# Two modes chains in turn, loads in source order, stores by POOL, and the residual made beside the first images

## The chip, the cores and the metric

The kernel runs on one core of a Trainium2 chip. The metric is the device time of one execution in microseconds; lower is better. Engines are TensorE (PE, with its weight loads as PEld), VectorE (DVE), ScalarE (ACT), GpSimd (POOL), and SyncE (SP), which here only issues DMAs. [...]

## The reference, cut to what matters

Two layers over an input of 256 x 256 x 128. Layer 0 is attention over rows; its result is x1, kept in DRAM as x1d. Layer 1 treats every one of 256 tokens as an image of 256 x 128 pixels (b*C tokens, H, W), and is a Fourier neural operator:

```python
attn = fno_layer(attn, p_wr, p_wi, p_bias, p_sw, p_sb, (H, W))
attn = instance_norm(attn + tokens, attn_norm_w, attn_norm_b)
attn = attn.reshape(b * (C // TOKEN_CODIM), TOKEN_CODIM, H, W)
h0 = instance_norm(attn, norm2_w, norm2_b)
h1 = fno_layer(h0, mix_wr[0], ..., norm=True, act=True)
h2 = fno_layer(h1, mix_wr[1], ..., norm=True)
out = instance_norm(h2, mon_w, mon_b) + attn
...
x = x + _L1_conv_ref(_gn(x), ...)
```

In the kernel's words: y is the unnormalized attn, an image per token; `lam` is its normalization's scale. Each fno_layer of the mixer is a spectral part (few Fourier modes: a transform, a product with weights, a transform back) and a skip part (a 4 x 4 channel mix). The first gives h1 with a Gelu ("first images"), the second h2. The output is `x1 + lam*y + kap*(h2's sums) + c0`, with kap and c0 from the statistics of h2.

## The kernel before, in words

Tokens are 256; on 128 partitions they make two halves, a = 0 and 1. Pixels of an image (32768) are cut into 16 blocks of NB = 2048, and these into 32 half blocks (units) of HB = 1024. `blocks` (16 tiles `hb[b]`) holds one half's whole image set in SBUF, 16 MB; it is used for half 0 first and for half 1 after that. Everything else goes through DRAM: x1d, `yd` (y), and mode tensors Gd0, Gd1, Gd2 (modes that are transformed back along one axis) and Yd (images that are transformed forward along one axis).

The parts, as Python generators or functions, each with `yield`s so that two can be woven:

- `y_blocks(a)` (L1280): for each unit u: load x1 of both halves (two 512 KB DMAs, tile `xt`, three slots in pool `xp`), for each even u the modes `gs` (four DMAs of Gd0); eight matmuls with `mpT` and the small `image` matmuls into four PSUM banks (`yps`); DVE scales them out (L1304) to `hb` (half 0) or a tile `yt` (half 1) and takes statistics (L1306); POOL stores y to yd (L1308) for half 1 and for b < 4 of half 0.
- `first_modes(a)` (L1374): DVE aggregates y's statistics, a chain of small operations makes lam, rho and sig; F (y's modes, from Fyd) is scaled; `mix_modes` multiplies with the weights (DVE products `x0m`, PE accumulates in `x0acc`), normalizes; `synth_modes` makes Gd1 in four chunks: matmuls `g10gp` into four banks, eviction by ACT and DVE to a tile `gt`, four stores of 256 KB to DRAM (L586, by SP).
- `first_images(a)` (L1411): for each block b: load modes `gs` (L1199), for half 1 also y (L1426, 1 MB); `ups` = skip + image matmuls, Gelu by ACT to `hb[b]` (L1446); then for block b-1: transposes `htps`, copies to `hT` (three by DVE at L1465, one by ACT at L1456), `sps` = skip of the second layer, of which DVE takes statistics (L1474), `psA` = transform along the width, copy by ACT, store to Yd (L1480, by SP). For half 0, `keep_y` stores y of blocks 4 to 15 to yd by POOL (L1432, 1 MB each) before `hb[b]` is overwritten.
- `second_modes(a)` (L1484): load `YT` from Yd in four chunks, transform (`f1ps`, L1513), `mix_modes` (`z0m`, `z0acc`), `synth_modes` to Gd2, then kap and c0 (`cvps`, L1535 to L1554).
- `second_images(a)` (L1556), the output blocks: load y, x1 (two DMAs of 512 KB each) and modes; `h2ps` = skip + image; ACT applies kap and c0 (L1583) in place; DVE makes x1 + lam*y (L1587) and adds hb (L1590); POOL stores to the output (L1591).

[...]In the mixer two pools of four are open at a time, so `ups` and `h2ps` share four, and `htps`, `sps` and `psA` share four.

The order at the end of the kernel (L1596 to L1635): y of half 0; first modes of half 0 woven with the first part of y of half 1; first images of half 0; second modes of half 0 woven with the rest of y of half 1; first modes of half 1 woven with output blocks of half 0; first images of half 1 woven with the rest of these; second modes of half 1; output blocks of half 1. `weave(main, side)` takes steps of the side generator when the numbers that main yields exceed those of the side.

`tc.manual_schedule(engines=COMPUTE)`: PE, ACT, DVE and POOL run their instructions in the order of the source; the order of SP's DMA issues is left to the scheduler, with its own estimate of due times. [...] A tile of a pool with `bufs=n` and one tag takes the n slots in turn; a load into a slot waits until its last user is done.

Of the kernel before, what the change touches and what calls it, by code (L numbers as in the profile page):

```python
# [10 lines left out]
FP = mybir.dt.float32  # L11
# [501 lines left out]
def layer1(tc, I, C, ident, x1d, upool, U, stats2, mv2, out):  # L513
# [9 lines left out]
    with ExitStack() as ctx:  # L523
# [16 lines left out]
        def synth_modes(pool, psum, Z, T, Gd, tag, spare=None, turned=False, chunk=None, ptag="s", gbufs=2):  # L540
# [4 lines left out]
            for c in range(4) if chunk is None else (chunk,):  # L545
                for part in range(1 if both else 2):
# [35 lines left out]
                    for ri in range(2) if both else (part,):  # L582
                        for jp in range(2):
                            k = 2 * ri + jp if both else jp
                            r0 = 16 * ri + 4 * c
                            nc.sync.dma_start(  # L586
                                Gd[r0 : r0 + 4, 2 * jp : 2 * jp + 2].rearrange("f j g t -> (j g) f t"),
                                gt[:, :, k * T : (k + 1) * T],
                            )
# [575 lines left out]
        END = 0.6  # L1165
# [52 lines left out]
        def flush(stage):  # L1218

            while next(stage, END) != END:  # L1220
                pass

# [7 lines left out]
        with tc.tile_pool(name="psb", bufs=4, space=PSUM) as psa, tc.tile_pool(name="spb", bufs=1) as spb:  # L1230
# [3 lines left out]
            ch4 = sp.tile([4, 6], FP, name="ch4")  # L1234
# [13 lines left out]
            for l in range(2):  # L1248
                s4 = sp.tile([4, 4], FP, name=f"s4_{l}")
# [4 lines left out]
                r4 = sp.tile([P, 4], FP, name=f"r4_{l}")  # L1254
# [14 lines left out]

        halves = []  # L1270
        for a in range(2):
# [6 lines left out]
            h.Yd = dram.tile([H, 32, P], FP, name=f"Yd_{a}")  # L1278

        def y_blocks(a, psum):  # L1280

            tt = slice(a * P, (a + 1) * P)
            for u in range(32):
                b, s = u // 2, u % 2
                xt = xts.pop((a, u)) if (a, u) in xts else load_x1(a, u)
                if s == 0:
                    gs = xp.tile([P, 4, P], FP, tag="gs", name=f"gs_{a}_{b}")
                    load_modes(gs, Gd0, b, tt)
                ps = [psum[0].tile([P, 512], FP, tag="y", name=f"yps_{a}_{u}_{j}") for j in range(4)]
# [8 lines left out]
                image(ps, gs, bsy, range(2 * s, 2 * s + 2))  # L1298
# [8 lines left out]
                if a or b < 4:  # L1307
                    nc.gpsimd.dma_start(ydv[:, a, u * HB : (u + 1) * HB], yt)  # L1308
                yield END

        def mix_modes(wp, psum, F, l, tag, out, constant=()):

# [3 lines left out]
            acc = [psum.tile([P, 512], FP, tag="q", name=f"{tag}acc_{r}") for r in range(2)]  # L1316
            by_c = [z.rearrange("p (c t) -> p c t", c=4) for z in acc]
            k = 0
            for i in range(4):
# [5 lines left out]
                for x, r, dst in ((0, "r", 0), (1, "n", 0), (0, "i", 1), (1, "r", 1)):  # L1325
                    t = wp.tile([P, 4, G, 4], FP, tag="m", name=f"{tag}m_{i}{x}{r}")
# [8 lines left out]
            sq = wp.tile([P, 2, 4, T], FP, tag="f", bufs=1, name=tag + "sq")  # L1335
# [4 lines left out]
            en = psum.tile([P, 512], FP, tag="q", name=tag + "ens")  # L1340
# [7 lines left out]
            rs = wp.tile([P, 2], FP, tag="rs", name=tag + "rs", bufs=1)  # L1348
# [4 lines left out]
            dg = wp.tile([P, P], FP, tag="m", name=tag + "dg")  # L1353
            nc.vector.tensor_scalar(dg, ident, rs[:, 0:1], None, ALU.mult)
            yield 1.8
            ps = psum.tile([P, 512], FP, tag="q", name=tag + "rsp")
# [5 lines left out]
            rsb = wp.tile([P, T], FP, tag="m", name=tag + "rsb")  # L1362
            nc.scalar.copy(rsb, ps[:, 0:T])
            Z = wp.tile([P, 4, 2, T], FP, tag="f", bufs=1, name=tag + "Z")
# [9 lines left out]
        def first_modes(a, wp, psum):  # L1374

            h = halves[a]
            F = wp.tile([P, 4, 2, P], FP, tag="F", bufs=1, name=f"F0_{a}")
# [4 lines left out]
            dg = wp.tile([P, 2, P], FP, tag="m", name=f"dg3_{a}")  # L1382
# [17 lines left out]
            ps = psum.tile([P, 512], FP, tag="q", name=f"rhops_{a}")  # L1400
            nc.tensor.matmul(ps[:, 0:256], ones, dg.rearrange("p k t -> p (k t)"), start=True, stop=True)
            yield 0.9
            rb = wp.tile([P, 256], FP, tag="m", name=f"rb_{a}")
# [7 lines left out]
            yield from mix_modes(wp, psum, F, 0, f"x{a}", z, ((sig, blk[0]), (ch[:, 2:3], ident)))  # L1411
            Z = z[0]
            for c in range(4):
                synth_modes(wp, psum, Z, P, h.Gd1, f"g1{a}", turned=True, chunk=c, ptag="q", gbufs=1)
                yield 2.7

        def first_images(a, wp, psk, pst):
# [5 lines left out]
            def load(b):  # L1423
                if a == 1:
                    ys[b] = wp.tile([P, NB], FP, tag="yt", name=f"y2_{a}_{b}")
                    nc.sync.dma_start(ys[b], ydv[:, a, b * NB : (b + 1) * NB])  # L1426
                gss[b] = wp.tile([P, 4, P], FP, tag="gs", name=f"gs2_{a}_{b}")
                load_modes(gss[b], h.Gd1, b)

            def keep_y(b):  # L1430
                if a == 0 and 4 <= b < 16:
                    nc.gpsimd.dma_start(ydv[:, a, b * NB : (b + 1) * NB], hb[b])  # L1432

            for b in range(4, 8):
                keep_y(b)
            load(0)
            for b in range(17):
                if b < 15:
                    load(b + 1)
                if b < 16:  # L1440
                    keep_y(b + 8)
                    ps = [psk.tile([P, 512], FP, tag="k", name=f"ups_{a}_{b}_{j}") for j in range(4)]
                    skip(ps, by_turn(ys.pop(b) if a else hb[b]), h.bl0, False)
                    image(ps, gss.pop(b), bs4)
                    for j in range(4):
                        nc.scalar.activation(by_turn(hb[b])[:, j], rows_of(ps[j]), AF.Gelu)  # L1446
                if b > 0:
                    turned = by_turn(hb[b - 1])
                    hT = {}
                    for j in (1, 2, 3, 0):  # L1450
                        ps = pst.tile([P, 512], FP, tag="t", name=f"htps_{a}_{b}_{j}")
# [18 lines left out]
                if b > 0:  # L1470
                    ps = [pst.tile([P, 512], FP, tag="t", name=f"sps_{a}_{b}_{j}") for j in range(4)]
# [3 lines left out]
                    psA = pst.tile([P, 512], FP, tag="t", name=f"psA_{a}_{b}")  # L1475
# [4 lines left out]
                    nc.sync.dma_start(  # L1480
# [4 lines left out]
        def second_modes(a, wp, psum):  # L1485
# [3 lines left out]
            F = wp.tile([P, 4, 2, P], FP, tag="F", bufs=1, name=f"F1_{a}")  # L1489
# [12 lines left out]
            gbufs = 1 if a == 0 else 2  # L1502
            load(0)
            yield 6.0
            for c in range(4):
                if gbufs > 1 and c < 3:
                    load(c + 1)
                ps = psum.tile([P, 512], FP, tag="q", name=f"f1ps_{a}_{c}")
# [11 lines left out]
                if gbufs == 1 and c < 3:  # L1520
                    load(c + 1)
                    yield 4.0
            z = []
            yield from mix_modes(wp, psum, F, 1, f"z{a}", z)
            Z, left = z
            for c in range(4):
                synth_modes(wp, psum, Z, P, h.Gd2, f"g2{a}", chunk=c, ptag="q", gbufs=gbufs)
                yield 2.7

            Fw = wp.tile([P, 2, P], FP, tag="m", name=f"Fw_{a}")  # L1530
            nc.vector.tensor_scalar(Fw, F[:, 0], hw0, None, ALU.mult)
            ps = psum.tile([P, 512], FP, tag="q", name=f"cvps_{a}")
# [6 lines left out]
            cv = wp.tile([P, P], FP, tag="m", name=f"cv_{a}")  # L1539
            nc.vector.tensor_mul(cv, blk[1], ps[:, 0:P])  # L1540
            yield 0.9
            ps = psum.tile([P, 512], FP, tag="q", name=f"cvps2_{a}")
# [13 lines left out]
        def second_images(a, wp, psk, bufs):  # L1556

            h = halves[a]
            lam, kap, c0 = (h.col[:, k : k + 1] for k in (3, 8, 9))
            got = {}  # L1560

            def load(b):
                xt, yt = [], []
                for s in range(2):
                    px = slice(b * NB + s * HB, b * NB + (s + 1) * HB)
                    yt.append(wp.tile([P, HB], FP, tag="yo", name=f"y4_{a}_{b}_{s}", bufs=bufs[1]))
                    nc.sync.dma_start(yt[s], ydv[:, a, px])
                    xt.append(wp.tile([P, HB], FP, tag="xo", name=f"x4_{a}_{b}_{s}", bufs=bufs[0]))
                    nc.sync.dma_start(xt[s], x1v[:, a, px])
                gs = wp.tile([P, 4, P], FP, tag="gs3", name=f"gs3_{a}_{b}")  # L1570
                load_modes(gs, h.Gd2, b)
                got[b] = xt, yt, gs

            load(0)
            for b in range(16):
                if b < 15 and bufs[1] > 3:
                    load(b + 1)
                xt, yt, gs = got.pop(b)
# [223 lines left out]
```

## Time and profile before

Three runs took 3005.37, 3007.17 and 3008.3 us. The profiled execution took 3009.91 us, with a span of 3007.9 us at a mean granted PE clock of 0.931.

| what | busy us, whole span | share |
|---|---|---|
| PE | 2638.8 | 88% |
| DVE | 2038.8 | 68% |
| POOL | 1514.7 | 50% |
| ACT | 1435.4 | 48% |
| DMA, bytes moved | 430.02 MB | mean 143 GB/s |

How to read it: these are means over parts with different limits. Layer 0 runs from the start to about 1656 us, the head of layer 1 (attention over tokens) to about 1905, and the parts named above fill the last 1100 us. A row of a table by stages has the stretch, its length, then busy time and instruction count of each engine, the granted PE clock, the busy share of the DMA engines and what they moved. A row of the chain of waits has a start, a length, and the engine and line (or the transfer) that held the end up at that time.

### The profile page before, as it was taken

To read this page: it belongs to the slowest core of one execution; us is meant where nothing else is said; L and a number is where in the kernel's file an instruction comes from. 1 tells how busy PE (TensorE), PEld (TensorE's weight loads), DVE (VectorE), ACT (ScalarE), POOL (GpSimd) and SP (SyncE) were. 2 spreads that over 40 slices of the span, in tenths; PEclk is the share of its full clock that TensorE was granted. 3 is DMA by queue.
4 is the path that set the end of the run, shared out by engine and by line. 5 is a ranking of instruction groups with operands and counts; after the bars stand their busy time and mean duration, and the time that the engine had idled before them with its cause. 6 is when DMAs were issued, how large, how long until landed. Compare 5 with 4: busy or idle time off the path is not lost. (4 is left out here: it accounts for less than half of the span.)

```text
span 3007.9 us, 70049 instructions
## 1 busy us (share of the span) xinstructions
PE 2638.8 (88%) x28526; PEld 1908.8 (63%) x28526; DVE 2038.8 (68%) x3251; ACT 1435.4 (48%) x2828; POOL 1514.7 (50%) x1174
## 2 busy tenths in 40 slices
PE   6899999999999999999999899898779866577644
PEld 6677777777777777777777467685545543333432
DVE  7788888888888888888888547465445445456354
ACT  0477777777777777777776223000132002343022
POOL 0499999999999999999999002000100000000011
PEclk9999999999999999999999899999989887788755
DMA  9422222122222221222221011885844576995499
GB/s 364 156 64 66 65 72 66 64 68 70 66 65 72 66 66 64 72 66 66 65 73 45 23 50 53 288 280 193 303 175 153 203 258 231 300 321 201 130 374 338
DMA packets 270202, 430.02 MB, mean 143 GB/s; under 512 B 26102, under 2 KB 202697, under 8 KB 262072
## 3 DMA queue, kind: packets, MB, share of 16 engines
q1 hardware_dynamic: 253176, 358.41, 35.8%
q0 software_dynamic: 16704, 67.12, 5.5%
q8 instruction: 226, 3.70, 0.5%
q14 instruction: 96, 0.79, 0.1%
HBM read 290.17 MB, written 135.27 MB: 141 GB/s over the span
## 5 line engine op out<-in xcount | busy, mean ns | idle before, releaser
L299 POOL TENSOR_TENSOR e<-e,b1T 128x1024 f32<-128x1024 f32 x256 | 606.5, 2369 | 166.1 <-PE u L348 90.5
L303 POOL TENSOR_TENSOR es<-e 128x512 f32<-128x512 f32 x512 | 639.0, 1269 | 20.1
L281 ACT ACTIVATE sc<-sc,b2T 128x512 f32<-128x512 f32 x512 | 339.0, 662 | 365.4 <-PE sc L272 357.1
L323 DVE RECIPROCAL av<-av 128x256 f32<-128x256 f32 x256 | 452.3, 1767 | 27.2 <-DVE og L322 1.4
L281 ACT ACTIVATE e<-sc,b2T 128x512 f32<-128x512 f32 x512 | 348.0, 680 | 0.0
L294 DVE TENSOR_TENSOR e<-sc,b1T 128x1024 f32<-128x1024 f32 x256 | 310.9, 1214 | 0.0
L272 PE MATMUL sc<-qkT 32*128 32x256 f32 x4096 | 294.0, 401 | 1.3 <-DVE e L294 1.3
L1591 POOL DMA_DIRECT2D out_dram<-x x64 | 34.0, 531 | 509.2 <-DVE x L1590 374.8
L1293 PE MATMUL yps<-xt,mpT 128*128 128x256 f32 x1024 | 251.7, 398 | 27.5 <-DVE yt L1304 24.5
L311 PE MATMUL av<-e,v 128*32 128x256 f32 x4096 | 274.8, 385 | 0.5 <-POOL e L299 0.5
L1308 POOL DMA_DIRECT2D yd<-yt x32 | 17.0, 531 | 479.3 <-DVE yt L1304 479.3
L272 PEld LDWEIGHTS sc<-qkT 32*128 32x128 f32 x4096 | 185.9, 185 | 112.1 <-issue 97.7
L1293 PEld LDWEIGHTS yps<-xt,mpT 128*128 128x128 f32 x1024 | 196.1, 197 | 72.2 <-DVE yt L1304 29.3
L322 DVE SCALAR_TENSOR_TENSOR og<-gate,av 128x256 f32<-128x256 f32 x256 | 107.7, 421 | 190.6 <-PE av L316 190.6
L327 POOL TENSOR_TENSOR x<-xt,bo 128x256 f32<-128x256 f32 x256 | 187.3, 732 | 0.0
L246 PE MATMUL qk<-xnT,wT_wq 128*128 128x256 f32 x512 | 179.6, 433 | 1.7 <-ACT xnT L238 1.7
L1583 ACT ACTIVATE blocks<-h2ps,col 128x512 f32<-128x512 f32 x128 | 89.1, 777 | 176.1 <-PE h2ps L1182 176.0
L252 PEld LDWEIGHTS gv<-wT_wv,kvT 128*128 128x128 f32 x1024 | 155.2, 192 | 13.2
L316 PE MATMUL av<-es,ones 128*32 128x256 f32 x2048 | 157.5, 379 | 2.5 <-POOL es L303 2.5
L333 PE MATMUL wo<-wT_wo,og 128*128 128x128 f32 x1024 | 156.9, 276 | 2.7 <-DVE og L324 2.7
L348 PE MATMUL u<-adft,x 128*128 128x129 f32 x1024 | 156.4, 275 | 0.0
L252 PE MATMUL gv<-wT_wv,kvT 128*128 128x128 f32 x1024 | 156.1, 275 | 0.0
(692 smaller groups left out, 5150.1 us busy)
## 6 DMA issues: line engine op xcount, KB each, us to landing
xt<-x1d SPq DMA_DIRECT2D x128, 512.0 KB
xb<-in_x_dram SPq DMA_DIRECT2D x32, 1024.0 KB
xt<-in_x_dram SPq DMA_DIRECT2D x128, 256.0 KB
kt<-in_L_conv_kv_x_dram SPq DMA_DIRECT2D x128, 256.0 KB
x1d<-x SPq DMA_DIRECT2D x256, 128.0 KB
y<-yd SPq DMA_DIRECT2D x64, 512.0 KB
x<-x1d SPq DMA_DIRECT2D x64, 512.0 KB
out_dram<-x POOLq DMA_DIRECT2D x64, 512.0 KB, 7.2
```

The lines of the kernel that those rows point to most:

```text
L246: nc.tensor.matmul(ps[:, 0:256], wT["wq"], xnT, start=True, stop=True)
L252: nc.tensor.matmul(ps[:, 256 + c * P : 256 + (c + 1) * P], kvT[:, c * P : (c + 1) * P], wT["wv"], start=True, stop=True,)
L272: nc.tensor.matmul(sc[h // 2][:, h % 2, c * 256 : (c + 1) * 256], qkT[p, 256 + c * P : 256 + (c + 1) * P], qkT[p, 0:256], start=True, stop ...
L281: nc.scalar.activation(r["e"][1][:, :, c, :] if hp else z, z, AF.Exp, bias=b2T[:, c, s : s + 1])
L294: nc.vector.tensor_tensor(r["e"][0].rearrange("p h c q -> p (h c q)"), r.pop("sc").rearrange("p h x -> p (h x)"), b1T[:, 0:2].rearrange("p ...
L299: nc.gpsimd.tensor_tensor(e1, e1, b1T[:, 2:4].rearrange("p h c q -> p (h c q)"), ALU.mult)
L303: nc.gpsimd.tensor_tensor(r["es"][hp], e[:, :, 0, :], e[:, :, 1, :], ALU.add)
L311: nc.tensor.matmul(ps[hd, 0:256], r["v"][:, c, hd], r["e"][h // 2][:, h % 2, c, :], start=(c == 0), stop=(c == 1),)
L316: nc.tensor.matmul(ps[32 * h : 32 * h + 32, 256:512], self.ones, r["es"][h // 2][:, h % 2, :], start=True, stop=True,)
L323: nc.vector.reciprocal(rd, rd)
L327: nc.gpsimd.tensor_tensor(r["x1"], r["x"], bc(self.bo, 1, 2), ALU.add)
L1293: nc.tensor.matmul(rows_of(ps[j]), mpT[:, sc, tt], by_turn(xt[:, sc])[:, j], start=(sc == 0), stop=False,)
```

## The change

- SP joins the manual schedule: its loads are issued in source order. Loads in `y_blocks` are written two units ahead. Stores that SP issued (Gd1, Gd2, Yd) are issued by POOL.
- x1 + lam*y of half 0 is made during its first images, for blocks b >= NW = 2: x1 is loaded (tile `xw` in the three `xt` slots), ACT scales y by lam into the tile's second half, POOL adds, and POOL stores the sum to a new DRAM tensor `wd`. `keep_y` is gone; yd of half 0 is stored for b < NW only. The output blocks of half 0 then load one w of 1 MB in place of y and x1, and DVE does one add per half block (for b < 2 as before).
- y of half 1: units 0 to 23 are woven with first modes of half 0 (weight 2.2 for 1.4), and run to the end before the first images; 24 to 31 are woven with the f1ps part of second modes of half 0.
- From there, second modes of half 0 and first modes of half 1 are stepped in turn, with no y beside them. They share the `m` (2) and `gt` (1) buffers. The first modes' synthesis is then woven with output blocks of half 0 (two chunks per block), and the first images of half 1 with the rest (weight 0.85 for 0.6). In that part y of half 1 and w share four slots of 1 MB.
- Half 1's output: y and x1 of the first NX = 5 half blocks are loaded, and x1 + lam*y made, during second modes of half 1; afterwards a load of the next half blocks is written after each output block, into five x slots and two y slots.
- `ch4`, `s4` and `r4` move from pool `sp` to `spb`.

On PE the order of instructions becomes: y of half 0; y of half 1 (24 units) with x0acc and g10gp between; 16 first images; 8 y units with f1ps; z0acc and x1acc in turn, g20gp, g11gp with two h2ps blocks, a third h2ps block; then 16 first images with 13 h2ps blocks between; f1ps to g21gp of half 1; 16 h2ps blocks.

The core of the diff (renamings of pools to `Banks` and `Tiles` are left out):

```diff
-        END = 0.6
+        NW, NX = 2, 5
...
-            ch4 = sp.tile([4, 6], FP, name="ch4")
+            ch4 = spb.tile([4, 6], FP, name="ch4")
...
+            load(lo)
+            load(lo + 1)
+            for u in range(lo, hi):
                 b, s = u // 2, u % 2
-                xt = xts.pop((a, u)) if (a, u) in xts else load_x1(a, u)
...
+                if u + 2 < hi:
+                    load(u + 2)
...
-                if a or b < 4:
+                if a or b < NW:
                     nc.gpsimd.dma_start(ydv[:, a, u * HB : (u + 1) * HB], yt)
...
+            def load_w(b):
+                for s in range(2):
+                    ys[b, s] = yp.tile([P, 2, HB], FP, tag="xt", name=f"xw_{b}_{s}", bufs=3)
+                    nc.sync.dma_start(ys[b, s][:, 0], x1v[:, a, b * NB + s * HB : b * NB + (s + 1) * HB])
...
+                    nc.scalar.activation(
+                        t[:, 1], hb[b][:, s * HB : (s + 1) * HB], AF.Identity, scale=h.col[:, 3:4]
+                    )
+                    nc.gpsimd.tensor_tensor(t[:, 1], t[:, 1], t[:, 0], ALU.add)
+                    nc.gpsimd.dma_start(wd[:, px], t[:, 1])
...
                 if b < 16:
-                    keep_y(b + 8)
...
                         nc.scalar.activation(by_turn(hb[b])[:, j], rows_of(ps[j]), AF.Gelu)
+                if a == 0 and NW <= b + 1 < 16:
+                    add_w(b + 1)
...
-                    nc.sync.dma_start(
+                    nc.gpsimd.dma_start(
                         h.Yd[16 * (b - 1) : 16 * b].rearrange("(n j) f t -> (j f) n t", j=4),
...
-        with tc.manual_schedule(engines=COMPUTE):
+        with tc.manual_schedule(engines=COMPUTE | {ENG.SP}):
...
+                U1 = 24
+                with tc.tile_pool(name="mp0", bufs=1) as wp:
+                    y1 = y_blocks(1, br, 0, U1)
+                    weave((2.2 * t for t in first_modes(0, wp, tiles(wp), bq)), y1)
                     run(y1)
+                with tc.tile_pool(name="hp0", bufs=2) as wp:
+                    run(first_images(0, wp, xp, bq, br))
+                with tc.tile_pool(name="mp1", bufs=1) as wp:
+                    y1 = y_blocks(1, br, U1, 32)
+                    m0 = second_modes(0, wp, tiles(wp), bq)
+                    weave((1.5 * t for t in iter(lambda: next(m0), None)), y1)
+                    run(y1)
+                    m1 = first_modes(1, wp, Tiles(F=(xp, "yt", 2), f=(xp, "yt", 2), m=(wp, "m", 2)), br)
+                    for _ in m0:
+                        next(m1)
+                    pools = [(xp, xp), 3, True]
+                    o0 = output_0(pools, bq)
+                    weave((t / 5.4 for t in m1), o0)
+                    pools[2] = False
+                    next(o0)
+            with tc.tile_pool(name="hp1", bufs=2) as wp, tc.tile_pool(name="op0", bufs=4) as op:
+                pools[:] = [(op, wp), 4, True]
+                weave((0.85 * t for t in first_images(1, wp, op, bq, br)), o0)
                 run(o0)
...
+                    m1 = second_modes(1, wp, tiles(wp), Banks(psq, "q"), gbufs=2)
+                    weave((0.3 for _ in m1), o1.ahead())
+                with tc.tile_pool(name="opk1", bufs=8, space=PSUM) as psk:
+                    o1.run(Banks(psk, "k"))
```

## The prediction, as put on record before the run

> **What bounds the kernel now.** I read the slices first, then the busy time of each stage, then the chain of waits and the queue's own waits in the stages that the diff rewrites. In the slices, the first 1.9 ms, attention and the head of layer 1, have 9s for PE and are untouched; the last slices, from about 1905 us, are what the diff rewrites, and PE's digits fall there:
>
> ```profile
> PE   6899999999999999999999899898779866577644
> ...
> DMA  9422222122222221222221011885844576995499
> ```
>
> The stages of that part, called B to H here, as busy time of each engine in its stretch (columns: stretch, length, PE, PEld, DVE, ACT, POOL, granted PE clock, DMA share, GB/s). A, the y blocks of half 0, fills 1905 to 2052 before them.
>
> ```profile
> 2052.00:2161.00 109.00, 89.81 (x972) 62.81 (x970) 57.41 (x138) 7.65 (x15) 6.37 (x12) 0.92 0.65 217
> 2161.00:2302.00 141.00, 117.92 (x1921) 61.69 (x1921) 70.72 (x113) 51.15 (x96) 6.84 (x13) 0.90 0.47 168
> 2302.00:2346.00 44.00, 35.62 (x452) 28.12 (x448) 18.63 (x42) 0.58 (x1) 3.19 (x6) 0.97 0.91 316
> 2346.00:2459.00 113.00, 91.42 (x740) 67.23 (x740) 56.12 (x130) 7.44 (x14) 6.37 (x12) 0.90 0.61 206
> 2459.00:2593.00 134.00, 61.97 (x1028) 35.57 (x1036) 63.48 (x95) 26.82 (x43) 7.97 (x15) 0.69 0.75 249
> 2593.00:2782.00 189.00, 148.76 (x2496) 73.53 (x2480) 109.63 (x146) 75.57 (x132) 9.56 (x18) 0.88 0.79 275
> 2782.00:2852.00 70.00, 44.35 (x596) 30.30 (x612) 23.55 (x46) 7.39 (x14) 0.00 (x0) 0.78 0.41 125
> 2852.00:3007.00 155.00, 73.90 (x1024) 44.02 (x1000) 78.63 (x75) 44.58 (x65) 17.00 (x32) 0.58 0.96 353
> ```
>
> B: first modes of half 0 beside 13 y units. C: first images of half 0. D1: the four f1ps chunks beside 6 units; D2: the rest of second modes beside 13 units. E: first modes of half 1 beside 7 output blocks; PE works 62 of 134 us, so this is a chain, not an engine. F: first images of half 1 beside 9 output blocks. G: second modes of half 1 alone. H: 16 output blocks, DMA full (0.96).
>
> E's chain of waits is DMA and SP, and SP's own waits there say why: loads wait for output stores and for the DVE add, and the Gd stores queue behind them.
>
> ```profile
> 2559.15 8.67 DMA out_dram<-x
> ...
> 2570.06 5.34 DMA Gd<-g11gt
> ...
> 2584.88 7.79 DMA gs<-Gd
> ```
>
> ```profile
> SPq L1569 <- DMA out_dram<-x: 35.8, 12, 6.4
> SPq L1567 <- DVE x L1587: 23.7, 10, 9.0
> ```
>
> F's chain, one block with an output block in it: PE waits for hstat, which waits on DVE behind the adds, which wait for ACT. From psA to psA this takes 15 us (2661.1 to 2676.0, the next one), a block without output 7.0.
>
> ```profile
> 2652.83 1.30 PE h2ps L1193 x32
> 2654.13 1.14 PE h2ps L1182 x32
> ...
> 2655.93 2.12 ACT blocks L1583 x3
> ...
> 2658.06 2.36 DVE x L1590 x2
> 2660.43 0.62 DVE hstat L1474
> ```
>
> [...]for the new 128x1024 add; the trace has 2.37 us for a TENSOR_TENSOR of that shape (L299), used here. [...]the trace has medians of 4.7 (yd<-yt) and 7.2 (out_dram, DMA full).[...]
>
> **The change, part by part** (against the profiled span, 3007.9; the three timed runs have a median of 3007.17, so no correction).
>
> 1. Start of A: ch4 and s4 now load after k_sel. Eight tiny issues at the 0.35 us of k_same and k_sel: **+3** (0 to +5). Nothing else changes in A: PE is full from 1960; two blocks of y stores fewer.
>
> 2. B has 24 y units instead of 13. A unit alone on four PSUM banks takes 4.87 us (2448.6 to 2453.5: 3.72 + 0.73 of PE and 0.5 of waiting for the DVE eviction). B began at 2049, 112 us with its first unit. Upper end: 112 + 11x4.87 = 166. Lower end: PE alone, 24x4.45 + 32 (rhops 0.6, x0acc 16, ens 2, g10gp 13) = 139. The new order puts y matmuls between all pairs of x0acc, so some of the 17 us in which PE idled fill up: 155, **+43** (+27 to +54). Gd stores move from SP to POOL, behind yd stores (0.53 us each): hidden, Gd1 isn't read until C, seven units later.
>
> 3. C. Removed: 12 yd stores of 1 MB in a burst at the start; PE lost 21.8 us there waiting for gs, queued behind them, so C without it is 141-23 = 118. Added, for 14 blocks: two x1 loads (SP), two ACT scalings of 128x1024, two POOL adds, two wd stores, and the Yd store moves behind these on POOL. ACT isn't the total bound, but its order is: both scalings stand between the gelus and the hT copy, on which the last sps quarter and psA wait. A scaling: 128x512 takes 0.58 to 0.68 here, so about 1.1; the 2.2 us push hT from 2210.9 to 2213.1 in the 6.97 us block, and psA's end by 1.6. 14x1.6 = 22. Second limit: three xt slots, each held for load 4.7 + issue 0.4 + POOL 2.4 + issue 0.5 + store 4.7 = 12.7, two per block: 8.5 us a block, against 8.6 by ACT. What queues behind a wait for a slot: on ACT the hT copy, so PE; on SP the next gs load, early enough. C = 118+22 = 140, **-1**. Lower end 118 (-23), if ACT's work fits in; upper end, see the third rival.
>
> 4. D1: 8 units and the f1ps chunks. Before, 44 us with 6 units, so 15 us of other time; 8x4.87+15 = 54, **+10** (0 to +15).
>
> 5. D2 and E. Before, 113 + 134 = 247. After: the two mode chains alternate with no y beside them. From the start: rho chain of half 1, as in B from bn_aggr to x0m, 17 us, with z0acc in it; rest of both mixes, ens and rs at PE's 1.02 us a product pair, until the first g20 chunk, about 41. Chunks share one gt buffer: evictions 1.3, four POOL issues 2.1, landing 3.6 (estimate: a 256 KB Yd store took 2.15, Gd stores 3.8 to 5.3) = 7 us each, four to 69; cvps and rsp lie beside. Then four g11 chunks, 28, plus 6 for an output block on ACT and DVE before the third eviction; then stores and gs load 10: 113. **-134** (-150 to -105). The 28 DVE multiply-adds of 1.25 us and the y loads that go from here and F are counted in this; in F they lay beside ACT's 2.8 us and were free.
>
> 6. F gets 13 output blocks instead of 9 (three stand in E). Each costs 15.1-7.0 = 8.1 more; the L1605 add stays in the same place in the chain. **+32** (+15 to +38). DMA: 16x1.5 + 13x2.25 MB in 221 us is 250 GB/s, no bound.
>
> 7. G: x1/y loads for five half blocks (5 MB) go between the YT loads on SP, and five 1.25 us adds stand in DVE's chain, before the F copies and inside the mix, where DVE has about 0.3 us of slack a product: **+6** (0 to +12).
>
> 8. H: five of 32 load pairs are gone, 5 MB at 353 GB/s, 15 us. But before, these loads began at 2852 while G's tail and the first block ran; with five x slots the next x load waits until the first output store has landed: after the gs load h2ps 2.4, ACT 3.1, adds 2.4, store 5, some 13 us. **0** (-15; +12 if two y slots slow the pace).
>
> Sum: 3+43-1+10-134+32+6+0 = **-41**: 2967.
>
> **Rivals.**
> - *It hides better.* ACT and POOL work in C fits beside PE and B runs at PE's floor: -22-16, 2929. For it: PE is full in C (94 of 94 us from 2206 to 2300) and ACT is busy for only 42 of these. Against: the order on ACT.
> - *Half given back.* The gt cycle stays at E's old pace, 10.2 us a chunk (41 us for four, 2535 to 2576): 8x3.2 = +26, and F at its upper end, +6: 2999. For it: one buffer for both chains. Against: SP's queue, which set that pace, no longer carries these stores.
> - *Slower: the ring of three slots in C.* C moves 2.6 MB a block; at 8.6 us that is 300 GB/s, as busy as D1 (0.91). With a load as slow as the 8.0 us of a queued YT load and a store of 7.2, a slot turns in 0.4+8.0+2.4+0.5+7.2 = 18.5, 12.4 us a block, C = 19+14x12.4 = 192: +52, 3019. It decides from a turn of about 17.4 us (11.6 a block, C at 181), where the gain of the rest is used up. Against: a slower ring asks for less bandwidth (2.6 MB in 12.4 us is 210 GB/s), which shortens the latencies.
> - That nothing happens is excluded: the order of instructions on all engines differs from 1905 on.
>
> **Chances.** Forecast 0.50 (2937 to 2997), hides better 0.24, half given back 0.12, ring 0.14. A measurement of this kernel can tell about 0.2%, 6 us, from no change. Faster: the first two and two thirds of the third, 0.81; same 0.06; slower 0.13. Range 2916 to 3019: below the second case's time by its own uncertain terms, up to the ring's; some 0.15 is left out.
>
> **What would show it.** First ups of half 0 at about 2207 (B); no 21.8 us gs wait and 8.6 us a block in C, with hT later on ACT; g20 and g11 chunks 7 us apart and the first ups of half 1 about 113 us after the last y unit; F at 15 us a block with output, some 220 in all; H as long as now, with DMA not full at its start. Wrong, if C's blocks are 7 or over 11 us apart, if F's output blocks cost other than 8 us, or if H shrinks by 15.

## The result, and the profile after

The changed kernel takes 3036.73 us (median of 4 runs) against 3006.84 us before: ratio 1.0102, 95% interval 1.0084 to 1.0119. It is slower; 2967 us was predicted. Run again unedited beside the last of the experiments it took 3037.05 us against 3002.45: ratio 1.0129 (1.0095 to 1.0163). The profiled span is 3033.0 us, 25.1 above the span before.

The slices after. PE's last fourteen digits were 98779866577644 before and DMA's 85844576995499: PE has gained nothing in these stages, and DMA has 98 in the last two slices, in H, where it had 99.

```profile
PE   6899999999999999999998999897898665776644
...
DMA  9322222222222222222221013786978727875498
```

The stages after, as busy time of each engine in its stretch (columns as in the prediction's table). The rows are B, C, D1, D2 with E, F, G, H; each ends with its last PE instruction, H with the span:

```profile
2050.30:2213.60 163.30, 135.06 (x1336) 101.44 (x1336) 88.29 (x202) 8.93 (x16) 24.32 (x39) 0.98 0.75 262
2213.60:2353.50 139.90, 128.10 (x1924) 59.73 (x1920) 73.30 (x118) 79.44 (x123) 93.88 (x72) 0.99 0.80 270
2353.50:2421.00 67.50, 46.54 (x512) 35.78 (x512) 21.27 (x49) 0.59 (x1) 4.51 (x8) 0.87 0.79 261
2421.00:2564.20 143.20, 85.92 (x1087) 52.01 (x1089) 62.94 (x131) 23.15 (x41) 27.64 (x39) 0.76 0.44 143
2564.20:2787.80 223.60, 165.71 (x2752) 81.09 (x2752) 98.91 (x138) 86.11 (x147) 25.36 (x41) 0.85 0.70 245
2787.80:2870.40 82.60, 47.30 (x580) 32.44 (x580) 29.42 (x52) 7.83 (x14) 12.64 (x17) 0.74 0.50 163
2870.40:3033.00 162.60, 75.49 (x1024) 44.30 (x1024) 73.26 (x72) 44.77 (x65) 17.08 (x32) 0.53 0.84 304
```

With the same boundaries on the profile before (us; misses are measured minus predicted change):

| stage | before | after | change | predicted | miss |
|---|---|---|---|---|---|
| start and A | 2049.0 | 2050.3 | +1.3 | +3 | -2 |
| B | 112.1 | 163.3 | +51.2 | +43 | +8 |
| C | 141.0 | 139.9 | -1.1 | -1 | 0 |
| D1 | 43.9 | 67.5 | +23.6 | +10 | +14 |
| D2 and E | 246.7 | 143.2 | -103.5 | -134 | +30 |
| F | 187.7 | 223.6 | +35.9 | +32 | +4 |
| G | 71.2 | 82.6 | +11.4 | +6 | +5 |
| H | 156.3 | 162.6 | +6.3 | 0 | +6 |
| sum | 3007.9 | 3033.0 | +25.1 | -41 | +66 |

What the two-chain stretch no longer carries came back elsewhere: 103.5 us gained, 110.7 paid in B, D1 and F for the y units and output blocks, 17.7 in G and H. Where the misses of D1 and E lie is in the waits. D1, on SP's order (start, duration, what was issued): after the last load for C nothing until the YT load, and x1 for the y units behind it; then PE in the same place:

```profile
2338.97 0.35 SPq L1456 DMA_DIRECT2D xw<-x1d  x1
2357.45 1.18 SPq L1531 DMA_DIRECT2D YT<-Yd  x2
2358.74 1.01 SPq L997 DMA_DIRECT2D xt<-x1d  x2
```

```profile
2352.40 1.07 PE L1513 MATMUL psA<-hT,k_bfwd 128*32 128x512 f32 x8
2368.15 1.19 PE L1316 MATMUL yps<-xt,mpT 128*128 128x256 f32 x2 [14.69 <-DMA xt<-x1d]
```

SP's own waits in D1 name the releaser (total, times, longest): the YT load waits for the last Yd store, which POOL issues at the end of C.

```profile
SPq L1531 <- DMA Yd<-yA: 17.8, 2, 14.7
```

In E the chain of waits reaches back to 2532.5 only. No wait for an output store stands ahead of the Gd stores any more, as it did before. The chain holds a wait for the shared gt buffer (the last g11 chunk is evicted when the store of the one before it has landed) and, at the end, the landing of an output store:

```profile
2532.51 7.06 DMA Gd<-g11gt
...
2539.67 1.08 ACT g11gt L581 x2
...
2553.61 3.24 DMA out_dram<-w
2556.85 0.02 SPq L1199
```

SP's waits in E say how long that last store held the first load of modes of half 1's images:

```profile
SPq L1199 <- DMA out_dram<-w: 12.5, 1, 12.5
```

On DVE in E, half 1's normalisation (rq_ve from x1ens; PE had ended x1ens at 2487.0) stands behind the last g20 eviction, which waits for gt:

```profile
2489.70 1.29 DVE L581 COPY g20gt<-g20gp 128x512 f32<-128x512 f32 x2 [6.67 <-DMA Gd<-g20gt]
2498.82 1.29 DVE L581 COPY g20gt<-g20gp 128x512 f32<-128x512 f32 x2 [7.84 <-DMA Gd<-g20gt]
2500.03 0.15 DVE L35 TENSOR_SCALAR rq_ve<-x1ens 128x1 f32<-128x1 f32 x1
```

F's chain for an output block is the one of before: ACT's four scalings, DVE's adds, hstat, psA. PE's psA takes 1.93 us here, 1.07 where PE is busy (above, end of C).

```profile
2584.38 2.78 ACT blocks L1600 x4
...
2588.32 1.22 DVE w L1605
2589.53 0.62 DVE hstat L1510
...
2590.20 1.93 PE psA L1513 x8
```

### The profile page after: what moved, and what is told of

Read it like the earlier page. It is cut to its first block, busy times and chain, and to the rows that moved or that the text cites. A ratio compares the mean times of both kernels' runs of the same rounds, so it can differ in the third digit from the quotient of the medians.

```text
span 3033.0 us, 70180 instructions
## 1 busy us (share of the span) xinstructions
PE 2657.6 (88%) x28526; PEld 1909.9 (63%) x28526; DVE 2004.9 (66%) x3223; ACT 1466.3 (48%) x2856; POOL 1661.2 (55%) x1310
## 5 line engine op out<-in xcount | busy, mean ns | idle before, releaser
L252 PEld LDWEIGHTS gv<-wT_wv,kvT 128*128 128x128 f32 x1024 | 155.0, 192 | 13.4
L311 PEld LDWEIGHTS av<-e,v 128*32 128x32 f32 x4096 | 107.0, 109 | 76.1 <-POOL e L299 1.0
```

Source lines behind the costliest of these rows:

```text
L252: nc.tensor.matmul(ps[:, 256 + c * P : 256 + (c + 1) * P], kvT[:, c * P : (c + 1) * P], wT["wv"], start=True, stop=True,)
L311: nc.tensor.matmul(ps[hd, 0:256], r["v"][:, c, hd], r["e"][h // 2][:, h % 2, c, :], start=(c == 0), stop=(c == 1),)
```

## The experiments

Edits are to the changed kernel unless said otherwise. Ratios are to the kernel before, timed beside each of them (its medians 2998.8 to 3004.5 us); the changed kernel's own are 1.0102 and 1.0129. Their intervals, 1.0084 to 1.0163 over both, overlap those of the single waits below, so that what a single wait is worth is read from stage lengths. These are from one profile each. The unedited kernel's second profile has its stages within 2 us of the first, but for B, which takes 5.5 us longer. In the profiles of the changed kernel's variants whose edit leaves a stage alone, B takes 163.3 to 171.6 us, D1 64.5 to 68.6, E (last y unit to first ups) 142.9 to 146.1, F 222.6 to 225.4, G 80.3 to 85.7, H 159.3 to 166.0. A difference within these ranges shows nothing, and neither do some 5 us of a whole span.

> The changed kernel unedited. Every theory: 3028 to 3037 us, its ratio to the kernel before 1.008 to 1.012 as when first timed, stages within 3 us of its first profile.

**Single waits.** First, the y loads ahead of YT in SP's order (a yield behind `load(lo + 1)`):

```
     y1 = y_blocks(1, br, U1, 32)
+    next(y1)
     m0 = second_modes(0, wp, tiles(wp), bq)
```

> The changed kernel with one move: the first two loads of x1 and the first load of modes of the y units beside half 0's second modes are put ahead of the first YT load in SP's order. Theory (SP's order made the stall): the YT load waits on SP for the last Yd store to land and holds the y loads behind it, so PE idled 14.7 us before the first of these y units; with the move it goes, the stretch from the last psA of half 0 to the last of the 8 y units falls from 68 to about 54 us and the whole from 3036.7 to about 3022. Rival (the transfers made it: three xt slots still held by the scaled blocks, and a DMA that the end of the images fills): the y loads start no earlier, or come in no earlier, and the time stays within 4 us of the changed kernel's.

Ratio 1.0090 (1.0063 to 1.0117), span 3024.6: -8.4. D1 falls to 59.9, -7.6. SP's order made the stall, but only half comes back: the x1 of the third unit is still written behind the YT load, is issued after it, and comes in beside it.

```profile
2353.86 1.07 PE L1514 MATMUL psA<-hT,k_bfwd 128*32 128x512 f32 x8
2354.86 3.72 PE L1317 MATMUL yps<-xt,mpT 128*128 128x256 f32 x16
...
2369.37 1.19 PE L1317 MATMUL yps<-xt,mpT 128*128 128x256 f32 x2 [5.26 <-DMA xt<-x1d]
```

```profile
2359.70 1.18 SPq L1532 DMA_DIRECT2D YT<-Yd  x2
2361.00 1.01 SPq L997 DMA_DIRECT2D xt<-x1d  x2
```

Then SP's order left to the scheduler:

```
-    with tc.manual_schedule(engines=COMPUTE | {ENG.SP}):
+    with tc.manual_schedule(engines=COMPUTE):
```

> The changed kernel with SP's order left to the scheduler again, as in the kernel before; the order on PE, DVE, ACT and POOL is as in the changed kernel. Theory (source order on SP made the stall ahead of half 1's last y units, 7.6 of whose microseconds came back when the y loads went first, and the late loads at the hand-over to half 1's images): both shrink, whole -8 to -18 us from 3036.7. Rival (these are waits for memory that any order of SP meets): within 4 us; or the scheduler puts loads ahead that wait for stores, and the whole is 5 to 15 us slower.

Ratio 1.0071 (1.0055 to 1.0086), span 3021.0: -12. D1 56.9 (-10.6): here the x1 of three units goes ahead of YT. G -2.4 lies within the spread and H -4.5 at its edge, and the two chains take 4 more: the hand-over did not shrink. The theory holds for D1 alone.

One output block fewer ahead of half 1's images. In this run the last output blocks of half 0 are formed from data that half 1's images have already overwritten; only its time is read.

```
-    pools = [(xp, xp), 3, True]
+    pools = [(xp, xp), 3, False]
     weave((t / 5.4 for t in m1), o0)
     pools[2] = False
-    next(o0)
```

> The changed kernel with two output blocks of half 0 instead of three ahead of the first images of half 1; the third moves into these images, which then hold 14. Theory (a new wait at the hand-over: the first load of modes of half 1's images goes into memory that the third block's store still reads, and so stood on SP until 2556.9, 8.5 us after the last g11 store had landed): from the last g11 eviction to the first ups 24.5 us falls to about 16, and the images grow by the 8.1 us of one output block: together -1 to +2 us against 3036.7. Rival (the chunks alone set this point, the store's wait only ran beside them): the hand-over stays at 24 us, the images grow by 8, the whole is +8 us.

Ratio 1.0134 (1.0107 to 1.0162), span +0.9. From the last g11 eviction to the first ups 19.5 in place of 24.5, F +5.8. So the third block's store does hold the first load, for some 5 us (this takes 22.9 to 25.2 in the profiles that leave it alone), not 8.5: the second block's store then does the same.

```
-    with tc.tile_pool(name="hp1", bufs=2) as wp, tc.tile_pool(name="op0", bufs=4) as op:
+    with tc.tile_pool(name="op0", bufs=4) as op, tc.tile_pool(name="hp1", bufs=2) as wp:
```

> The changed kernel with the two pools of half 1's images and of the outputs beside them opened in the other order, so that the first tiles of the images lie elsewhere. Theory (the first load of modes of these images stood on SP until the third output block's store had read the memory it goes to, 8.5 us after the last g11 store landed): over other memory it goes when g11 has landed, the last g11 eviction to the first ups takes 15 to 18 us in place of 24.5, whole -5 to -8 us. Rival (SP's next load in order, w or y, then waits for the same store, or the tiles fall on memory that is used as late): 22 us or more, whole within 3 us.

Ratio 1.0110 (1.0088 to 1.0132), span +0.2. The first load of modes still waits for the same store; my reason, where its tiles lie, is not supported, and why that load waits for it stays open.

The gt buffer in halves (YT, which shares the memory, too):

```
-    gt = pool.tile([P, 4, 512], FP, tag="gt", ..., bufs=gbufs)
+    hf = [pool.tile([P, 4, 256], FP, tag="gt", ..., bufs=2 * gbufs) for ri in range(2)]
...
+    hf[ri][:, f, :], ps[f][:, 256 * ri : 256 * ri + 256]
```

> The changed kernel with each gt buffer (and each YT buffer, which shares its memory) as two halves of half the size, evicted, stored and freed by themselves; 8 evictions of 128x256 a chunk in place of 4 of 128x512. Theory (one shared buffer, held from its eviction to the landing of its store, sets the pace of the chunks: 8.0 to 9.1 us each for g20, 8.1 to 11.3 for g11): with halves in turn a chunk takes 5.5 to 6.5 us, so 12 to 16 us go from the stretch between the last y unit and the first ups of half 1 (142 us now), 2 to 3 from half 1's second modes; whole about 3020. Rival (the chain of the chunks is PE, evictions and the issue on POOL, 3.0 us a chunk, and what waits is hidden by the other chain): the chunks stay at 8 us or more, whole within 4 us of 3036.7 or up to 6 slower by the added evictions.

Ratio 1.0097 (1.0068 to 1.0126), span -5.4. First evictions of successive g11 chunks are 6.5, 6.4 and 8.6 us apart in place of 8.4, 8.1 and 11.3; the stretch is 7.2 us shorter; G, 2.2 shorter, lies within the spread. The buffer does set the pace, by half of what I expected.

Half 1's first modes one step further ahead:

```
-    for _ in m0:
+    for i, _ in enumerate(m0):
         next(m1)
+        if i == 3:
+            next(m1)
...
     weave((t / 5.4 for t in m1), o0)
+    next(o0)
```

> The changed kernel with half 1's first modes one step further ahead in the turns (one more step of it after the fourth), so that its normalisation on DVE stands behind three g20 evictions in place of four; the three output blocks stay ahead of half 1's images, the first of them after the third g11 chunk instead of the second. Theory (on DVE, in order, that normalisation waits for evictions that wait for gt: rq at 2500.2, although x1ens was ready at 2487): it comes a chunk earlier, from the first g20 to the first g11 eviction 38 us falls to about 30, the whole stretch from 142 to 134 to 137, whole -5 to -8 us. Rival (the chunks of both chains share one buffer anyway, so that an earlier g11 only pushes the last g20 behind it): first ups no more than 3 us earlier, whole within 3 us of 3036.7.

Ratio 1.0152 (1.0130 to 1.0175), span 3046.6: slower by 13.6. The first g20 eviction comes 58 us after the last y unit (53 before the edit), so half 1's normalisation is ready only 3 us earlier (76 in place of 79), and two output blocks now lie in the hand-over, 34 us in place of 24.5. Neither theory has it: with one order for two chains, a step taken early by one is taken late by the other.

The idea itself undone: half 0's second modes to their end, then half 1's.

```
-    for _ in m0:
+    for _ in range(len(list(m0))):
         next(m1)
```

> The changed kernel with the idea at its centre undone alone: half 0's second modes run to their end before half 1's first modes begin, and no y unit or output block is put between; the rest stays (three output blocks at the same places of half 1's modes). Theory (two chains in turn hide each other's waits, but share one gt buffer, DVE[...]): the stretch from the last y unit to the first ups of half 1 grows from 142 us to about 165 (33 to the first g20 eviction, 33 for four chunks, 47 to the first g11 eviction, 27 for the others, 24.5 to the images), whole +18 to +28 us from 3036.7. Rival (the chains meet on DVE and on the shared buffer, so that in turn they hide nothing): within 6 us.

Ratio 1.0173 (1.0139 to 1.0207), span +10.7; the stretch takes 156.6 in place of 143.2. Taking turns is worth 13 us, not 23.

**The end.** The five early load pairs behind f1ps:

```
-    weave((0.3 for _ in m1), o1.ahead())
+    run(iter(lambda: next(m1), None))
+    weave((0.6 for _ in m1), o1.ahead())
```

> The changed kernel with the five pairs of loads of half 1's outputs and their five adds put behind the f1ps chunks of half 1's second modes (from the mix on) instead of among the YT loads and F copies. Theory (these loads share the DMA with YT and stand ahead of it on SP, and the first add stands ahead of an F copy on DVE): the stretch from the last first-image block to the last f1ps falls from 31 us to about 24 as in the kernel before; the mix has the adds still; whole -6 to -9 us from 3036.7. Rival (only moved: the loads and adds then delay the mix or the first output block by as much): within 3 us of 3036.7.

Ratio 1.0093 (1.0065 to 1.0121), span -0.2. G -6.6, outside the spread; H +4.4, 1 us above what H takes elsewhere with nothing changed in it. The profiled execution was the slowest of its six (3036.09 us, their median 3027.93). Whether the gain of G is only moved, as the rival has it, stays open. Then the rings at the end with the sizes of before (`late` is a pool opened after G):

```
-    y = self.wp.tile([P, HB], FP, tag="yo", ..., bufs=2)
+    y = (self.wp if k < NX or k % 4 < 2 else self.late).tile([P, HB], FP, tag=f"yo{...}", ..., bufs=1)
-    x = self.wp.tile([P, HB], FP, tag="xo", ..., bufs=NX)
+    x = (self.wp if k % 6 < 5 else self.late).tile([P, HB], FP, tag=f"xo{k % 6}", ..., bufs=1)
```

> The changed kernel with six x and four y slots for half 1's outputs, as the kernel before has, in place of five and two (the five loaded ahead stay as they are). Theory (the smaller rings set the pace of the last stage: 4.74 us a half block with the DMA engines 0.91 to 0.96 busy, before 4.33 with 1.03): from the first h2ps of half 1 to the last 150 us falls to 138 to 144, whole -6 to -12 us from 3036.7. Rival (each load waits for the landing of an output store that was issued just before it, whatever the number of slots, or the DMA engines set the pace): 148 or more, whole within 3 us.

Ratio 1.0095 (1.0081 to 1.0110), span -5.7; the h2ps stretch takes 146.3 us in place of 151.0, and 147.8 to 153.7 in the other profiles with this end and SP in source order. Alone that is at the edge of the spread. Beside the scheduler's SP order, which alone gives 146.6, the rings give 141.4 and 142.2 (the two runs with edits together, below). So the slots seem to be a part of the pace, not all of it.

**F.** The late adds of half 0's outputs on POOL:

```
-    nc.vector.tensor_tensor(w[s], w[s], hb[b][...], ALU.add)
+    (nc.vector if a or b < 3 else nc.gpsimd).tensor_tensor(w[s], w[s], hb[b][...], ALU.add)
```

> The changed kernel with the 26 last adds of half 0's outputs (128x1024, those beside half 1's first images) on POOL in place of DVE. Theory (an output block costs these images 8 us because hstat, on which psA waits, stands on DVE behind two adds that wait for ACT's four scalings): a block with output falls from 15 to 10 to 12 us, the images from 224 us to 165 to 190, whole -35 to -55 us from 3036.7. Rival (the block is set by ACT, or by PE at its low granted clock, and DVE's adds only lay in the way of nothing; POOL at 2.4 us an add then delays the stores): images 215 us or more, whole -8 to +10 us.

Ratio 0.9988 (0.9973 to 1.0004), span 2991.7: -41. F is 184.7 us. Is that DVE's load, or the adds' place in its order? The adds again on DVE, issued behind the four hstat:

```
-    for s in range(2):
-        nc.vector.tensor_tensor(w[s], w[s], hb[b][...], ALU.add)
-        nc.gpsimd.dma_start(outv[:, a, px], w[s])
+    late_adds.append((a, b, w))
...
         nc.vector.bn_stats(hstat[:, 4 * (b - 1) + j, :], ps[j])
+    if a:
+        flush_adds()
```

> The changed kernel with the 26 late adds of half 0's outputs left on DVE, but issued behind the four hstat of the block instead of ahead of them. Theory (it is their place: in order on DVE, hstat and with it psA waited behind adds that wait for ACT's four scalings): psA no longer waits for hstat, images of half 1 from 224 us to 185 to 200, whole -24 to -39 us. Rival (behind hstat they stand ahead of the next block's hT copies, which then wait for ACT in their stead, and psA with them): images 215 us or more, whole within 9 us. Only another engine then helps.

Ratio 0.9990 (0.9970 to 1.0010), F 183.6: the place alone does it. The chain of this run in F is PE, hstat no longer behind an add, and a block that waits for no load takes 9.4 us (2651.70 to 2661.13) in place of 15:

```profile
2651.70 1.15 PE ups L1193 x32
2652.85 1.11 PE ups L1182 x32
2653.96 1.90 PE htps L1489 x16
2655.86 1.29 PE h2ps L1193 x32
2657.15 1.10 PE h2ps L1182 x32
2658.25 1.03 PE sps L1193 x27
...
2659.31 0.71 DVE hstat L1510
...
2660.07 1.06 PE psA L1515 x8
2661.13 1.09 PE ups L1193 x32
```

The waits in F say the same (total, times, longest). The changed kernel, then the run with the adds behind, where PE's own wait for hstat ahead of psA has shrunk from 55.1 us to 7.6, again twelve times, and loads begin to count:

```profile
PEld psA L1513 <- DVE hstat L1510: 69.6, 16, 5.6
...
DVE w L1605 <- ACT blocks L1600: 55.6, 12, 4.7
PE psA L1513 <- DVE hstat L1510: 55.1, 12, 4.7
```

```profile
DVE hstat L1510 <- PE sps L1193: 41.8, 17, 9.7
...
PE ups L1193 <- DMA y<-yd: 31.1, 8, 16.1
```

**On the kernel before.** One part of the change alone, x1 + lam y beside half 0's first images (`load_w`, `add_w` as in the diff, w read back in the output blocks):

> The kernel before with one part of the change alone: x1 + lam y of half 0 made beside its first images (scaling on ACT, add on POOL, store to DRAM) and read back as w in its output blocks; the stages, their weights and SP's order by the scheduler stay. Theory (this part is free in the first images, where it takes the place of the burst of y stores, and shortens the output blocks, whose y and x1 loads queued ahead of the Gd stores): first images of half 0 at 140 us as before, the first modes of half 1 with seven output blocks down by 5 to 20 of 134 us, images of half 1 the same; whole -5 to -20 us from 3000 to 3007. Rival (the loads did not set that stage, or w adds more to the first images than the burst cost): within 4 us, or up to 15 slower.

Ratio 0.9996 (0.9984 to 1.0009). C 141.1, E 6.4 us shorter, F 188.7 as before, other stages up by as much: the rival. Then the 18 late adds alone on POOL, with the edit of above (`b < 7`):

> The kernel before with one edit: the last adds of half 0's outputs from block 7 on (18 of 128x1024, those beside half 1's first images) on POOL in place of DVE. Theory (the wait of hstat behind these adds costs each output block in these images 3 to 4 us whatever is done elsewhere): images of half 1 from 188 us to 150 to 165, whole -20 to -35 us from 3000 to 3007. Rival (here the multiply-adds of 1.25 us stay on DVE and keep hstat late, or ACT's scalings do): within 6 us.

Ratio 0.9949 (0.9935 to 0.9963); F 169.5 in place of 187.7: 18 us off, where I expected 23 to 38. Both together:

> The kernel before with x1 + lam y made beside half 0's first images (as in the run of that part alone) and the 18 late adds on POOL. Theory: images of half 1 have neither multiply-add nor add on DVE: 188 us to 150 to 160, the first modes of half 1 some 6 us shorter as in that run; whole 2965 to 2978 us. Rival (the images are set by PE at the granted clock once DVE's wait is gone, so that removing the multiply-adds too brings nothing): the same as the kernel before with the adds alone on POOL, within 4 us.

Ratio 0.9882 (0.9855 to 0.9909), 2964.01 us; F 152.3. Taking the multiply-adds and their loads from F, worth nothing as long as the adds stood ahead of hstat, is worth 17 us once they don't. PE is now full there (140.32 of 152.30, clock 0.94):

```profile
2588.30:2740.60 152.30, 140.32 (x2496) 75.22 (x2496) 69.20 (x111) 75.15 (x131) 52.94 (x36) 0.94 0.83 291
```

**The edits together, on the changed kernel.** Four edits (scheduler's SP order, halves, adds on POOL, rings), then six (one step ahead and pool order too):

> The changed kernel with four of the edits tried singly: SP's order by the scheduler, gt in halves, the 26 adds of half 0's late outputs on POOL, six x and four y slots at the end. Theory (they act in different stages, so their differences of profiled spans add: -12, -5, -41, -6): 2965 to 2985 us against the 3000 to 3007 of the kernel before. Rival (what one frees another takes: the images without DVE's wait run into the DMA engines[...]): 2986 to 2997, as with the adds alone.

> The changed kernel with all edits that were tried singly on it: SP's order by the scheduler, gt in halves, late adds on POOL, six x and four y slots, half 1 one step ahead, pools in the other order. Theory (each removes a wait of its own): 8 to 14 us below the 2973.8 of the first four together, 2960 to 2966, level with the kernel before with w beside and adds on POOL (2964.0): the idea brings no more than it costs. Rival (its waits hid a gain): below 2955. Rival (the last two edits meet what the others already gave): 2970 to 2976.

Ratios 0.9922 (0.9895 to 0.9950) and 0.9899 (0.9877 to 0.9920), 2973.77 and 2971.76 us. The four add up, -66.2 of span against -64 summed. The last two, which alone had not helped, bring nothing that can be told: the intervals overlap, and from the first ups of half 0 to the end the six take 757.0 us, the four 748.7 (F is 190 in place of 178). Both kernels beat before and after. The arrangement of before, with w beside and the adds on POOL, has the lowest time of all, 2964, though its interval overlaps that of the six. So with these waits taken out, the changed arrangement is level with that of before, not ahead of it; what SP's order, gt in halves or the rings leave to gain in the latter was not run.

## Why the prediction was wrong, step by step

**Step 5 failed, and with it the sign.** It put D2 and E at 113 us; 143 were measured, 30 of the 66 us missed. Its terms, from the last y unit: to the first g20 eviction "about 41", measured 52.8. The two chains' products and half 1's rho chain share DVE in one order, so the 22 small operations of rho, and then half 1's products, stood between z0's products instead of beside them (DVE worked 18 of the first 25 us). The run not in turn shows it: with half 1's steps gone from between, the first g20 eviction comes after 29.4. The chunks, "7 us each", are 8.0 to 9.1 for g20. The term "then four g11 chunks" had no wait between: g11 began 13 us after the last g20 chunk, 38.2 from first g20 to first g11 in place of 28, and half 1's normalisation stood behind evictions that waited for gt. That order is read in the trace; that it is the cause is not shown, since the one edit aimed at it took 3.3 us off these 38.2 and made the whole stretch longer. The stores and gs load, 10 and one chunk, took 24.5 in place of 17; 5 of these were the wait for an output store (the run with two output blocks). The edit to gt gave 7 us back, so the buffer was the term it was named for, mis-sized.

**Step 4 failed.** "44, 8 units and 15 us of other time" reads D1 as work; it was SP's order. The YT load waits for POOL's last Yd store, and the loads for all eight y units are queued behind it: PE idle 14.7 us. I had listed what the change moves to POOL and that SP is in source order, and did not walk SP's queue through this join. Moving two units' loads gave 7.6 back, the scheduler's order 10.6 of the 14 that this step missed.

**Step 2** is at the upper end of its range, 51 against 43, and above it, at 57, in the second profile. "Some of the 17 us in which PE idled fill up" did not happen: these waits, for evictions of y units (10.3) and for products (6.6), are now 26.8 (14.8 and 12.0). In the new order a product of the mix stands on DVE behind the eviction and the statistics of the y unit just ahead of it, which DVE can begin only when PE has ended that unit. PE's timeline shows the wait three times alike:

```profile
2092.40 1.12 PE L1351 MATMUL x0acc<-x0m_10i,ident 128*128 128x512 f32 x2 [3.40 <-DVE x0m_10i L1350]
...
2103.62 1.63 PE L1351 MATMUL x0acc<-x0m_20i,ident 128*128 128x512 f32 x2 [3.40 <-DVE x0m_20i L1350]
...
2116.52 1.13 PE L1351 MATMUL x0acc<-x0m_30i,ident 128*128 128x512 f32 x2 [3.40 <-DVE x0m_30i L1350]
```

**Step 3** was right: 139.9 against 140, 8.7 us a block on average, and the burst's wait for gs is gone. Its mechanism held too: psA's weight loads wait for ACT's hT copy 22.5 us in all, 22 were forecast. The 28 adds on POOL took 2.36 us each, as assumed. The ring rival did not come. The argument against it, that transfers land sooner where less is moved, is in the profile before: yd<-yt stores of 512 KB landed in a median of 8.7 us in D1, at 316 GB/s, and in 4.5 and 4.2 in B and D2, at 217 and 206.

**Step 6** was right in size, +36 against +32. But it took 15 us a block as a property of the block. It was the adds' place on DVE, and seeing that in F's chain, which the prediction quotes, would have shown where the larger gain lay.

**Steps 7 and 8** were too low by 5 and 6. In G two pairs of y and x loads stand ahead of YT loads on SP, and PE waited 17.6 us for YT (13.4 before); f1ps took 6.4 us more, and 24.2 in place of 31.8 with these pairs put behind it. The mix took 2.9 more. In H the early pairs did help, the first output store coming 7.0 us after c0 in place of 14.7, but the 31 intervals between the stores take 4.74 us in place of 4.33: 12.6 us. The slots may explain a part.

**The rivals.** "Half given back", gt at 10.2 us, was nearest in E: the mean was 8.8. The slower outcome that I priced, the ring in C, was the wrong one. What came in the main was one mechanism, an instruction behind another's wait in the same queue: on SP in D1 and G, where edits show it (7.6 and 10.6 us in D1, 6.6 in G), and on DVE in B and E, where the run not in turn shows it for the first part of E (29.4 us in place of 52.8) and the rest is read from the trace (three waits of 3.40 us in B). None of my rivals was of that kind. The chance of 0.81 for faster rested on treating two chains as parallel. Without the 30 us missed in D2 and E the change would have come out 5 us ahead.

## What to carry to other kernels

When two chains are written in turn, walk every engine's queue, SP's too, through each join. In this kernel the loads of the last y units stood on SP behind a YT load that waited 14.7 us for a store, and SP's order alone cost about as much (12 us of span) as the turns saved (13 us). Before moving work away from a stage, ask why it costs there what it does: the output blocks were 15 us each because two adds stood ahead of hstat, and changing that place alone took 40 us, about what the whole rearrangement was forecast to bring. Edits gate each other: taking the same multiply-adds away was worth 0 us in that stage with the adds in the way and 17 without, so a part that measures as nothing isn't shown to be worthless.

## What the runs showed of the hardware

On DVE an operation waited for the one written ahead of it: with the adds moved behind hstat, on the same engine with the same load, F went from 223.6 us to 183.6. What I had not expected is that the psA behind a wait of PE also ran longer. In the changed kernel's F its eight matmuls took 1.93 to 1.94 us in 12 of the 16 blocks, each time after a wait of 3.5 to 4.7 us, and 1.06 to 1.07 in the four blocks without a wait just before them. The granted clock was 0.50 over each of the twelve (2590.2 to 2592.1 is the first) and 1.00 over each of the four (2661.1 to 2662.2 is the first); over all of F it was 0.85, and 0.91 with the adds moved. There psA took 1.06 to 1.07 us in 15 of 16 blocks, after waits of at most 0.74 us; in the sixteenth, 1.94 after 0.74, PE had waited 3.27 us for gs 6.5 us earlier. Gd and Yd stores issued by POOL occupied it for 0.75 to 0.76 us each against 0.53 for most of the output stores, so that four for one chunk hold POOL for 3.0 us.
